# Eight half products and four small steps moved from ahead of the first attention to beside it, with the list steps of the last attention reordered

## The chip, the cores and the metric

The kernel runs on one core of one Trainium2 chip. The core has a matrix engine (PE, with its weight loads shown apart as PEld), a vector engine (DVE), a scalar engine (ACT), GpSimd (POOL) and a queue engine (SP) that issues most transfers. The metric is the device time of one execution in microseconds; less is better.

## The reference

The input is `x` (4 sequences of 512 tokens, 256 wide) and `cond_8` (4 by 8). All arithmetic is float32.

```
# 1. conditioned FFN: one of 8 experts for each sequence
e   = argmax(cond_8[b])
h   = silu(x[b] @ W_up[e].T + b_up[e]) * (x[b] @ W_gate[e].T + b_gate[e])   # 512 x 512
co  = h @ W_down[e].T + b_down[e]                                         # 512 x 256
# 2. attention with 16 query heads of 16 and one key/value head
q = (co @ Wq.T + bq) / 4;  k, v = split(co @ Wkv.T + bkv)
x = x + (softmax(q @ k.T) @ v) @ Wo.T + bo
# 3. a linear layer whose weight is mixed for each sequence
w_bot = sum_g cond_8[b, g] * weight[g] * mask
z = x @ w_bot.T + bias
# 4. mixture of 8 experts, two for each token, 128 places for each expert and group of 256 tokens
logits = z @ w_router;  probs = softmax(logits);  top 2
x = x + sum_e probs[e] * (gelu(z @ wi[e]) @ wo[e])     # places in order of choice, then token
```

The conditioned FFN's second product, `h @ W_down[e].T`, is what `down` computes. The mixed weight `w_bot` of each sequence is turned and multiplied by `w_router` once (`turn_mixed`, `route_mixed`), so that the logits come out of the same product as `z`.

## The kernel before, in words

The order of the work on every engine is the order of the program text; nothing rearranges it. Waits between engines come from the tiles that instructions share.

PSUM has eight banks of 128 x 512 floats in three groups: three `m`, one `a`, four `x` (`bank`). A product that wants a bank waits until the engine that reads the bank's last content is done.

**Ahead of the first attention.** For each sequence b and each quarter hc of the hidden width, `hidden(b, hc)` makes two products (lines 279 and 281), a silu on ACT (283) and an add and multiply on DVE (284) into the tile `hid`. `down(b, dc)` multiplies the whole of `hid` by one half of the output width (line 263, four products of 512 columns) and ACT adds the bias (264) into `coT`. `mixed` adds up the mixed weights on DVE (250, 252), four at a time. `keys`, `queries` and `values` project the sequence (313, 328, 335). For sequence 3, the last one, the four `hidden` and the `down` of sequences 2 and 3 stand in a table `before_steps`, together with turns (693) and routes (705) of the mixed weights: entry m runs after the maxima of step m, for m from 0 to 5. A large fill of the scatter buffer `xp` with zeros is issued from ACT's queue (361) just before.

**The attention steps.** 64 steps, 16 for each sequence, numbered n = 16 b + k. A step n handles the maxima of step n + 6 (`maxima`, four products at line 375 of 32 rows each, so that four fit the array side by side, and four DVE reductions, 379) and the exponentials of step n (`exponentials`, four products at 404 and four ACT exponentials, 408), and adds the weighted values of step n - 1 (`weigh`, line 422: products of 32 output columns, four side by side, accumulated in the `a` bank over four steps). After every fourth weighing the bank is copied out (431): by ACT, but by DVE for the last two units, 14 and 15. `shifted` turns the maxima (387) and sends them by four small transfers into rows of `q` (391). The last six steps (58 to 63) have no maxima left.

A step has one of two orders. Where the step's side work has PE products, it is called dense: half of the maxima and exponentials, the side work, the other half, then both halves of the weighing. Otherwise it is plain: half of the maxima and exponentials, half of the weighing, the other half of each, with the side work before the last half of the weighing.

**Side work.** The tables `beside` (sequences 0 to 2) and `last` (sequence 3) name, for each k, pieces of other sequences by their offset: projections of the next sequence, and of the previous ones the loads (`values`), the inverse sums (472), the residual bias (493, 128 x 1024 on DVE), the normalising (485), the output products (502, 507), turns (523), the mixed linear layer (534, 538), the choice of experts (`choose`, `rank0`, `rank1`, line 551 to 590), their places (`places`, `rows`, lines 600 to 631), `send` (637 to 649) and the scatter of rows to `xp` (`row0` to `row3`, line 655, two POOL transfers each). `bias` needs the residual rows that `residual` loads at steps 0, 27, 43 and 56.

In the last attention also stand the parts of `first_pairs`: lists of the first units of two tiles of 128 rows that belong to one expert (lines 826 to 879, some 14 to 18 small DVE instructions), the fetch of their weights (911) and rows (933), and the turn of unit 0 (975, 977).

**The experts.** Then come 25 units, of 256 or fewer rows each: `up` (1048, 1052), `put` (1081, 1091), and an accumulating scatter on POOL (1095). Weight tiles have three buffers. The pieces of the last sequence stand between the first units.

**Memory.** `hid` has two buffers in the pool `cp`, which is closed with `c1` ahead of the steps; the pools `ep`, `rp` and `fp` then take that room.

Of the kernel before, what the change touches and what calls it, by code (L numbers as in the profile page):

```python
# [10 lines left out]
F32 = mybir.dt.float32  # L11
# [6 lines left out]
P = 128  # L18
# [24 lines left out]
def adaln_attn_ffn_kernel(  # L43
# [77 lines left out]
    qp = attn_ctx.enter_context(tc.tile_pool(name="qp", bufs=2))  # L121
    c1 = ExitStack()
# [135 lines left out]
    def down(b, dc):  # L258
        w = w_of[b][1]
        wd = w[:, 0:1024].rearrange("p (c d) -> p c d", c=4)  # L260
        po = bank("x")
        for hc in range(4):
            mm(po, wd[:, hc, ts(dc, P)], hid_of[b][:, hc, :], start=hc == 0, stop=hc == 3)  # L263
        nc.scalar.activation(
            coT[:, dc, ts(b, T)], po, AF.Identity, bias=w[:, 1032 + dc : 1033 + dc]
        )

    def hidden(b, hc):
# [5 lines left out]
        if hc == 0:  # L274
            hid_of[b] = cp.tile([P, 4, T], F32, name="hid")
# [120 lines left out]
    def exponentials(n, js):  # L396
# [4 lines left out]
        for n4, j in enumerate(js):  # L401
            px = bank("m" if n4 >= 2 else "x")
# [10 lines left out]
    def weigh(n, js):  # L413
# [7 lines left out]
        for hh in range(4):  # L421
# [3 lines left out]
                start=sc == 0 and j0 > 0, stop=sc == 3 and j0 == 0,  # L425
# [273 lines left out]
    def route_mixed(b):  # L699
# [28 lines left out]
        [(-1, "bias"), (-2, "row1")],  # L728
# [8 lines left out]
        [],  # L737
# [6 lines left out]
        [(-1, "inv"), (0, "pairs0")],  # L744
        [(-1, "bias"), (-2, "send"), (-2, "row0")],
        [(-1, "norm0"), (-1, "norm1"), (-2, "row1")],
        [(-1, "out0"), (-1, "out1"), (-1, "out2"), (-1, "out3"), (-2, "row2")],
        [(-1, "rT0"), (-1, "rT1"), (-2, "row3")],
        [(-1, "mix0"), (-1, "mix1"), (-1, "mix2"), (-1, "mix3")],
        [(-1, "choose"), (-1, "rank0")],  # L750
        [(-1, "rank1"), (0, "pairs1")],
        [(-1, "places"), (-1, "rows"), (-1, "send"), (-1, "row0")],
        [(0, "values0"), (0, "pairs2"), (-1, "row1")],
        [(0, "pairs3"), (-1, "row2")],
        [(0, "bias"), (-1, "row3")],
        [(0, "pairs4")],
# [12 lines left out]

    def side(b, k):  # L770

        for off, name in (last if b == B - 1 else beside)[k]:
# [14 lines left out]

    before_steps = [
        [(hidden, B - 1, 0), (down, B - 2, 0)],
        [(down, B - 2, 1), (hidden, B - 1, 1), (turn_mixed, 0), (turn_mixed, 1)],  # L790
        [(hidden, B - 1, 2), (route_mixed, 0), (route_mixed, 1), (turn_mixed, 2)],
        [(hidden, B - 1, 3), (route_mixed, 2), (turn_mixed, 3)],
        [(down, B - 1, 0), (route_mixed, 3)],
        [(down, B - 1, 1)],
# [12 lines left out]
    fp = attn_ctx.enter_context(tc.tile_pool(name="fp", bufs=2))  # L807
# [8 lines left out]
    pairs = fp.tile([P, NE + 1], F32, name="pairs", bufs=1)  # L816
# [508 lines left out]
```

## Time and profile before

The median of 7 runs is 651.32 us (649.08 to 652.66). The profiled execution took 649.74 us, with a span of 647.9 us. The columns are busy times in us.

| stretch (us) | what runs | PE | DVE | ACT | DMA share |
|---|---|---|---|---|---|
| 0 to 69 | conditioned FFNs 0 to 2, first projections | 67.29 | 27.29 | 14.55 | 0.64 |
| 69 to 109 | FFN 3, `down` 2 and 3, turns, routes, maxima 0 to 5 | 40.00 | 24.16 | 7.06 | 0.71 |
| 109 to 171 | attention of sequence 0 | 62.00 | 42.19 | 39.74 | 0.13 |
| 171 to 239 | attention of sequence 1 | 68.00 | 47.23 | 38.13 | 0.24 |
| 239 to 306 | attention of sequence 2 | 66.96 | 50.57 | 36.93 | 0.28 |
| 306 to 361 | attention of sequence 3 to step 57 | 53.95 | 43.85 | 28.48 | 0.23 |
| 361 to 385 | steps 58 to 63, start of unit 0 | 21.63 | 14.69 | 15.24 | 0.66 |
| 385 to 625 | experts | 239.98 | 81.47 | 44.59 | 0.74 to 0.96 |
| 625 to 648 | last products and adds | 7.19 | 3.36 | 1.09 | 0.14 |

A product in float32 is two instructions on PE, so counts of PE instructions are twice those of products (transposes are single). The ends of PE instructions are modelled, and a PE instruction that is held up inside a group of products can look busy; the distance between the starts of the same instruction in two steps is the safer reading. In a line of the timeline, the bracket at the end gives the engine's idle time before it and what ended it.

### The profile page before, as it was taken

How to read it: one execution, taken by the hardware profiler on the slowest of the kernel's cores; microseconds unless marked ns; L12 is line 12 of the kernel's file. 1: busy time of each engine (PE TensorE's matmuls, PEld its weight loads, DVE VectorE, ACT ScalarE, POOL GpSimd, SP SyncE). 2: the span in 40 equal slices, each digit the busy share in tenths (PEclk: the TensorE clock that was granted, in tenths of full speed). 3: DMA queues.
4: the chain of work that ended last, by engine and by line, in shares of the span. 5: the costliest groups of instructions: out<-in, count | busy, mean ns of one | idle time of the engine just before them, and what ended most of it. 6: DMA issues, size and time to landing. Idle time of an engine off the chain costs nothing.

```text
span 647.9 us, 10621 instructions
## 1 busy us (share of the span) xinstructions
PE 627.0 (97%) x3968; PEld 373.2 (58%) x3968; DVE 334.8 (52%) x831; ACT 225.8 (35%) x404; POOL 111.3 (17%) x146
## 2 busy tenths in 40 slices
PE   8999999999999999999999999999999999999990
PEld 3444454333333433344335368888899999778880
DVE  1174844677668677876896853458222221322320
ACT  1212123566655455654553741221111111111220
POOL 1600000000000000310013051215342222223332
PEclk9999999999999999999999999999999999999996
DMA  6953981300142204321033299636889999898711
GB/s 232 379 146 71 310 268 34 98 19 18 34 133 68 67 18 119 133 70 47 19 97 122 95 344 305 220 99 197 249 270 324 315 340 318 249 278 256 215 20 19
DMA packets 65405, 107.14 MB, mean 165 GB/s; under 512 B 6914, under 2 KB 26946, under 8 KB 65346
## 3 DMA queue, kind: packets, MB, share of 16 engines
q1 hardware_dynamic: 50066, 87.96, 41.4%
q0 software_dynamic: 6400, 8.72, 6.8%
q10 hardware_dynamic: 8880, 9.71, 4.8%
q8 instruction: 33, 0.54, 0.3%
q14 instruction: 26, 0.21, 0.1%
HBM read 79.59 MB, written 26.65 MB: 164 GB/s over the span
## 4 chain that ended last, share of the span: by engine, by line
PE 91%; DVE 3%; DMA 2%; issue 1%; POOL 1%; SPq 0%; ACT 0%; POOLq 0%; DVEq 0%
PE ps_m L375 20%; PE ps_m L1048 17%; PE ps_x L1081 16%; PE ps_a L422 9%; PE ps_x L263 4%; PE ps_a L279 4%; PE ps_x L281 4%; PE ps_x L534 2%; PE ps_x L313 2%; PE ps_x L502 2%; PE ps_x L404 2%; PE ps_a L975 1%; PE ps_x L328 1%; PE ps_x L1015 1%; DVE negm L379 1%; PE ps_m L992 1%
## 5 line engine op out<-in xcount | busy, mean ns | idle before, releaser
L379 DVE TENSOR_REDUCE negm<-ps_m 128x1 f32<-128x512 f32 x250 | 160.7, 686 | 65.0 <-PE ps_x L404 43.1
L408 ACT ACTIVATE e<-ps_x 128x512 f32<-128x512 f32 x244 | 132.4, 594 | 106.0 <-PE ps_x L404 100.5
L375 PE MATMUL ps_m<-k,q 32*128 32x512 f32 x500 | 152.6, 639 | 0.4 <-DVE negm L379 0.3
L404 PE MATMUL ps_x<-q,k 32*128 32x512 f32 x488 | 138.9, 639 | 0.0
L1048 PE MATMUL ps_m<-xT,wi_sb 128*128 128x256 f32 (+1 forms) x672 | 115.4, 330 | 0.0
L1081 PE MATMUL ps_x<-wo_sb,e 128*128 128x256 f32 x512 | 114.3, 379 | 0.0
L1048 PEld LDWEIGHTS ps_m<-xT,wi_sb 128*128 128x128 f32 x672 | 103.7, 191 | 9.7 <-issue 0.4
L1081 PEld LDWEIGHTS ps_x<-wo_sb,e 128*128 128x128 f32 x512 | 95.6, 190 | 12.6 <-issue 0.4
L1052 ACT ACTIVATE e<-ps_m 128x512 f32<-128x512 f32 x64 | 38.0, 597 | 174.8 <-PE ps_m L1048 173.3
L1095 POOL DMA_INDIRECT out_dram<-y,to_row x36 | 55.5, 1542 | 137.1 <-DMA out_dram<-y,to_row 47.3
L375 PEld LDWEIGHTS ps_m<-k,q 32*128 32x128 f32 x500 | 46.4, 183 | 56.1 <-DVE negm L379 26.3
L422 PE MATMUL ps_a<-e,v 128*32 128x256 f32 x1024 | 75.8, 388 | 1.4 <-DVE cmp L826 1.4
L422 PEld LDWEIGHTS ps_a<-e,v 128*32 128x32 f32 x1024 | 23.2, 108 | 80.5 <-issue 64.0
L977 DVE COPY xT<-ps_a 128x256 f32<-128x256 f32 (+1 forms) x23 | 12.1, 528 | 82.1 <-PE ps_a L975 82.1
L1091 DVE TENSOR_SCALAR y<-ps_x,w 128x256 f32<-128x256 f32 x32 | 15.4, 483 | 58.8 <-PE ps_x L1081 58.7
L655 POOL DMA_INDIRECT xp<-x,to_i x32 | 33.2, 1038 | 57.6 <-DVE negm L379 29.7
L404 PEld LDWEIGHTS ps_x<-q,k 32*128 32x128 f32 x488 | 38.1, 182 | 2.1 <-issue 1.8
L584 POOL TENSOR_SCALAR x<-mk 128x4 f32<-128x4 f32 x4 | 0.8, 210 | 204.1 <-DVE mk L581 204.0
L284 DVE SCALAR_TENSOR_TENSOR hid<-ps_x,wo_sb,sg 128x512 f32<-128x512 f32 x16 | 12.0, 749 | 45.6 <-PE ps_x L281 45.6
L279 PE MATMUL ps_a<-xT_sb,wi_sb 128*128 128x512 f32 x64 | 30.5, 598 | 0.2 <-DMA wi_sb<-in_wcond_dram 0.2
L281 PE MATMUL ps_x<-xT_sb,wi_sb 128*128 128x512 f32 x64 | 30.1, 592 | 0.0
L263 PE MATMUL ps_x<-hid,wo_sb 128*128 128x512 f32 x64 | 28.8, 597 | 0.0
(166 smaller groups left out, 469.1 us busy)
## 6 DMA issues: line engine op xcount, KB each, us to landing
wi_sb<-in_wi_dram SPq DMA_DIRECT2D x25, 1024.0 KB
wo_sb<-in_wo_dram SPq DMA_DIRECT2D x25, 1024.0 KB
xp<-zeros ACTq DMA_DIRECT2D x1, 8712.0 KB
q<-qd SPq DMA_DIRECT2D x8, 512.0 KB
wi_sb<-in_wcond_dram SPq DMA_DIRECT2D x15, 256.0 KB
od<-stage SPq DMA_DIRECT2D x15, 256.0 KB
xt<-xp SPq DMA_DIRECT2D x11, 264.0 KB
wo_sb<-in_wcond_dram SPq DMA_DIRECT2D x4, 517.0 KB
```

What stands on the lines that cost most here:

```text
L263: mm(po, wd[:, hc, ts(dc, P)], hid_of[b][:, hc, :], start=hc == 0, stop=hc == 3)
L279: mm(pu, wu[:, c, :], xT_sb[:, c, ts(b, T)], start=c == 0, stop=c == 1)
L281: mm(pg, wg[:, c, :], xT_sb[:, c, ts(b, T)], start=c == 0, stop=c == 1)
L375: mm(pm, q[32 * j : 32 * j + 32, i, ts(hg, P)], k[32 * j : 32 * j + 32, :], start=True, stop=True,)
L379: nc.vector.tensor_reduce(nm[:, i, j : j + 1], pm, AX.X, ALU.max, negate=True)
L404: mm(px, k[rows_j, ts(sc, P)], seqs[u // 4]["q"][rows_j, :, ts(u % 4, P)], start=True, stop=True,)
L408: nc.scalar.activation(e_of[n][:, :, j, :].rearrange("p h (i t) -> p i h t", i=4), px.rearrange("p (i h t) -> p i h t", i=4, h=4), AF.Exp,)
L422: i = mm(pa_of[u][32 * hh : 32 * hh + 32, j0 * P : (j0 + nj) * P], seqs[b]["v"][:, sc, :], e[:, hh, j0 : j0 + nj].rearrange("p j n -> p (j ...
L1048: mm(ph[:, ts(k, n)], wi_of[u][:, c, ts(f0 + k, P)], xT_of[u][:, c, :], start=c == 0, stop=c == 1,)
L1052: nc.scalar.activation(hT_of[u][:, f0 : f0 + each].rearrange("p f t -> p (f t)"), ph, AF.Gelu_apprx_tanh,)
L1081: mm(po[:, 0:D], hT_of[u][:, fc, ts(h, P)], wo_of[u][:, fc, :], start=fc == 0, stop=fc == F // P - 1,)
L1095: i = nc.gpsimd.indirect_dma_start(out=out_rows, out_offset=bass.IndirectOffsetOnAxis(ap=to, axis=0), in_=y, in_offset=None, compute_op=AL ...
```

## The change

- `down` can take half of the tokens (256 columns). The eight halves of sequences 2 and 3 leave `before_steps` and stand in a table `halves` beside steps 3 to 9 and 11 of the first attention; the turns of the mixed weights of sequences 2 and 3 stand in step 12, their routes in step 13. These steps become dense.
- The hidden tiles of sequences 0 and 1 share one buffer; those of 2 and 3 get a pool `hp` of their own on the other side of the memory, closed at step 16. The pool `fp` and its first tiles are made there.
- In dense steps and in the last steps the weighing is one call over all four blocks of columns, products of 512 instead of 256 columns.
- In the steps without maxima the first two exponentials use `m` banks and the last two `x`, the other way round than before.
- The residual bias moves from step 5 of the next sequence (step 4 in the last attention) to step 14 of its own; that of the last sequence from 14 to 15.
- In `last`, `send` of sequence 1 moves from 4 to 3; the first list from 3 to 6; the second from 10 to 8; the fetches that stood with it stay at 10; `send` and `row0` of sequence 2 move from 11 to 12, `row1` from 12 to 13; the turn of unit 0 moves from 13 to 14.

```diff
@@ -119,6 +119,8 @@
     coT = apool.tile([P, 2, NT], F32, name="coT")
     wb_sb = apool.tile([P, B, 2, D + NE], F32, name="wb_sb")
     qp = attn_ctx.enter_context(tc.tile_pool(name="qp", bufs=2))
+    c2 = ExitStack()
+    hp = c2.enter_context(tc.tile_pool(name="hp", bufs=1, side="right"))
     c1 = ExitStack()
     cp = c1.enter_context(tc.tile_pool(name="cp", bufs=2))
     c1p = c1.enter_context(tc.tile_pool(name="c1p", bufs=1))
@@ -255,14 +257,20 @@
     mixing = [(b, g) for b in range(B) for g in range(NE)]
     hid_of = {}
 
-    def down(b, dc):
+    def down(b, dc, half=None):
+        n = T if half is None else T // 2
+        t0 = 0 if half is None else half * n
         w = w_of[b][1]
         wd = w[:, 0:1024].rearrange("p (c d) -> p c d", c=4)
-        po = bank("x")
+        po = bank("x")[:, 0:n]
         for hc in range(4):
-            mm(po, wd[:, hc, ts(dc, P)], hid_of[b][:, hc, :], start=hc == 0, stop=hc == 3)
+            mm(
+                po, wd[:, hc, ts(dc, P)], hid_of[b][:, hc, ds(t0, n)], start=hc == 0,
+                stop=hc == 3,
+            )
         nc.scalar.activation(
-            coT[:, dc, ts(b, T)], po, AF.Identity, bias=w[:, 1032 + dc : 1033 + dc]
+            coT[:, dc, ds(b * T + t0, n)], po, AF.Identity, bias=w[:, 1032 + dc : 1033 + dc]
         )
 
     def hidden(b, hc):
@@ -272,7 +280,11 @@
             for n in range(2)
         )
         if hc == 0:
-            hid_of[b] = cp.tile([P, 4, T], F32, name="hid")
+            hid_of[b] = (
+                cp.tile([P, 4, T], F32, name="hid", bufs=1) if b < B - 2
+                else hp.tile([P, 4, T], F32, name=f"hid{b}")
+            )
         pu = bank("a")
         pg = bank("x")
         for c in range(2):
@@ -399,7 +411,8 @@
         if n not in e_of:
             e_of[n] = ep.tile([P, 4, 4, P], F32, name="e")
         for n4, j in enumerate(js):
-            px = bank("m" if n4 >= 2 else "x")
+            px = bank("m" if len(js) == 4 and n4 < 2 else "x")
             rows_j = slice(32 * j, 32 * j + 32)
             mm(
                 px, k[rows_j, ts(sc, P)], seqs[u // 4]["q"][rows_j, :, ts(u % 4, P)],
@@ -422,7 +435,7 @@
             i = mm(
                 pa_of[u][32 * hh : 32 * hh + 32, j0 * P : (j0 + nj) * P], seqs[b]["v"][:, sc, :],
                 e[:, hh, j0 : j0 + nj].rearrange("p j n -> p (j n)"),
-                start=sc == 0 and j0 > 0, stop=sc == 3 and j0 == 0,
+                start=sc == 0 and js[-1] == 3, stop=sc == 3 and j0 == 0,
             )
         weighed.append(i)
         if sc == 3 and j0 == 0:
@@ -725,7 +738,7 @@
         [(-1, "values"), (1, "k"), (-2, "places"), (-2, "rows")],
         [(-2, "send")],
         [(-1, "inv"), (-2, "row0")],
-        [(-1, "bias"), (-2, "row1")],
+        [(-2, "row1")],
         [(-1, "norm0"), (-2, "row2")],
         [(-1, "norm1"), (-2, "row3")],
         [(-1, "out0"), (-1, "out1")],
@@ -734,26 +747,26 @@
         [(-1, "mix0"), (-1, "mix1")],
         [(-1, "mix2"), (-1, "mix3")],
         [(-1, "choose")],
-        [],
+        [(0, "bias")],
         [],
     ]
     last = [
         [(-2, "rank0")],
         [(-2, "rank1")],
         [(-1, "values"), (-2, "places"), (-2, "rows")],
-        [(-1, "inv"), (0, "pairs0")],
-        [(-1, "bias"), (-2, "send"), (-2, "row0")],
+        [(-1, "inv"), (-2, "send")],
+        [(-2, "row0")],
         [(-1, "norm0"), (-1, "norm1"), (-2, "row1")],
-        [(-1, "out0"), (-1, "out1"), (-1, "out2"), (-1, "out3"), (-2, "row2")],
+        [(-1, "out0"), (-1, "out1"), (0, "pairs0"), (-1, "out2"), (-1, "out3"), (-2, "row2")],
         [(-1, "rT0"), (-1, "rT1"), (-2, "row3")],
-        [(-1, "mix0"), (-1, "mix1"), (-1, "mix2"), (-1, "mix3")],
+        [(-1, "mix0"), (-1, "mix1"), (0, "pairs1"), (-1, "mix2"), (-1, "mix3")],
         [(-1, "choose"), (-1, "rank0")],
-        [(-1, "rank1"), (0, "pairs1")],
-        [(-1, "places"), (-1, "rows"), (-1, "send"), (-1, "row0")],
-        [(0, "values0"), (0, "pairs2"), (-1, "row1")],
-        [(0, "pairs3"), (-1, "row2")],
-        [(0, "bias"), (-1, "row3")],
-        [(0, "pairs4")],
+        [(-1, "rank1"), (0, "pairs2")],
+        [(-1, "places"), (-1, "rows")],
+        [(-1, "send"), (-1, "row0"), (0, "values0"), (0, "pairs3")],
+        [(0, "pairs4"), (-1, "row1"), (-1, "row2")],
+        [(0, "pairs5"), (-1, "row3")],
+        [(0, "bias"), (0, "pairs6")],
     ]
     ON_PE = ("q", "k", "v", "out", "rT", "mix")
 
@@ -767,8 +780,21 @@
     STEPS = 16 * B
     work = {b: finish(b) for b in range(B)}
 
+    halves = {
+        k: [(down, b, dc, half)]
+        for k, (b, dc, half) in zip(
+            (3, 4, 5, 6, 7, 8, 9, 11), itertools.product((B - 2, B - 1), range(2), range(2))
+        )
+    }
+    halves[12] = [(turn_mixed, 2), (turn_mixed, 3)]
+    halves[13] = [(route_mixed, 2), (route_mixed, 3)]
     def side(b, k):
 
+        for f, *of in halves.get(k, ()) if b == 0 else ():
+            f(*of)
         for off, name in (last if b == B - 1 else beside)[k]:
             to = b + off
             if not 0 <= to < B:
@@ -784,14 +810,9 @@
                 work[to][name]()
 
 
     before_steps = [
-        [(hidden, B - 1, 0), (down, B - 2, 0)],
-        [(down, B - 2, 1), (hidden, B - 1, 1), (turn_mixed, 0), (turn_mixed, 1)],
-        [(hidden, B - 1, 2), (route_mixed, 0), (route_mixed, 1), (turn_mixed, 2)],
-        [(hidden, B - 1, 3), (route_mixed, 2), (turn_mixed, 3)],
-        [(down, B - 1, 0), (route_mixed, 3)],
-        [(down, B - 1, 1)],
+        [(hidden, B - 1, 0)], [(hidden, B - 1, 1)], [(hidden, B - 1, 2)], [(hidden, B - 1, 3)],
+        [(turn_mixed, 0), (turn_mixed, 1)], [(route_mixed, 0), (route_mixed, 1)],
     ]
     for m in range(LEAD):
         maxima(m, (0, 1, 2, 3))
@@ -804,7 +825,6 @@
     c1.close()
     ep = attn_ctx.enter_context(tc.tile_pool(name="ep", bufs=2))
     rp = attn_ctx.enter_context(tc.tile_pool(name="rp", bufs=2))
-    fp = attn_ctx.enter_context(tc.tile_pool(name="fp", bufs=2))
 
 
 
@@ -813,12 +833,6 @@
     UHALF = NA + NB + NTILE
     UQUARTER = UHALF + NE
     NUNIT = UQUARTER + NE
-    pairs = fp.tile([P, NE + 1], F32, name="pairs", bufs=1)
-    nc.gpsimd.memset(pairs, 0.0)
-    texp = fp.tile([P, NUNIT], F32, name="texp", bufs=1)
-    table = fp.tile([P, 2, NUNIT], I32, name="table", bufs=1)
-    count = fp.tile([P, 1], I32, name="count", bufs=1)
     def of_experts(t, less, op, begin):
 
         n = begin.shape[2]
@@ -949,17 +963,19 @@
             next(parts[0])
         elif part == "1":
             next(parts[0], None)
+        elif part == "2":
             fetch_in(0)
             fetch_rows(0)
             fetch_rows(1)
-        elif part == "2":
+        elif part == "3":
             for _ in list_of_pairs(N0, NA - N0):
                 pass
-        elif part == "3":
+        elif part == "4":
 
             i = fetch_in(1)
             tc.add_manual_dep(i.ins, weighed[-1].ins.name, AFTER, reason="not at once")
             fetch_out(0)
+        elif part == "5":
             turn(0, "x")
         else:
             i = fetch_in(2)
@@ -1119,21 +1135,29 @@
 
     for n in range(STEPS + 1):
         m = n + LEAD
+        if n == 16:
+            c2.close()
+            fp = attn_ctx.enter_context(tc.tile_pool(name="fp", bufs=2, side="right"))
+            pairs = fp.tile([P, NE + 1], F32, name="pairs", bufs=1)
+            nc.gpsimd.memset(pairs, 0.0)
+            texp = fp.tile([P, NUNIT], F32, name="texp", bufs=1)
+            table = fp.tile([P, 2, NUNIT], I32, name="table", bufs=1)
+            count = fp.tile([P, 1], I32, name="count", bufs=1)
         if n in (0, 27, 43, 56):
             residual((0, 27, 43, 56).index(n))
         b, k = divmod(n, 16)
         names = [name for _, name in (last if b == B - 1 else beside)[k]] if b < B else []
         dense = any(
             name.rstrip("0123") in ON_PE and (b > 0 or name in projection[0]) for name in names
-        )
+        ) or (b == 0 and k in halves)
         if m >= STEPS:
             if n < STEPS:
                 exponentials(n, (0, 1, 2, 3))
             if n == STEPS:
 
                 up(0, 0)
-            weigh(n - 1, (2, 3))
-            weigh(n - 1, (0, 1))
+            weigh(n - 1, (0, 1, 2, 3))
             if n < STEPS:
                 side(b, k)
         elif dense:
@@ -1146,8 +1170,7 @@
             if m % 4 == 3:
                 shifted(m // 4)
             if n > 0:
-                weigh(n - 1, (2, 3))
-                weigh(n - 1, (0, 1))
+                weigh(n - 1, (0, 1, 2, 3))
         else:
 
             maxima(m, (0, 1))
```

## The prediction

> **What bounds the kernel now.** I read the page's busy line first, then the same busy times by stage, then the PE timeline of single steps, and last the stretch where PE has gaps.
>
> ```profile
> span 647.9 us, 10621 instructions
> PE 627.0 (97%) x3968; PEld 373.2 (58%) x3968; DVE 334.8 (52%) x831; ACT 225.8 (35%) x404; POOL 111.3 (17%) x146
> ```
>
> Columns of the next view: stretch, its length, then busy time and count on PE, PEld, DVE, ACT, POOL, the granted clock, DMA share and GB/s.
>
> ```profile
> 69.00:109.00 40.00, 40.00 (x164) 19.42 (x160) 24.16 (x43) 7.06 (x11) 0.11 (x1) 1.00 0.71 225
> 109.00:171.00 62.00, 62.00 (x514) 21.97 (x515) 42.19 (x69) 39.74 (x72) 0.00 (x0) 1.00 0.13 40
> 306.00:361.00 55.00, 53.95 (x432) 21.67 (x432) 43.85 (x102) 28.48 (x55) 8.99 (x11) 1.00 0.23 75
> 361.00:385.00 24.00, 21.63 (x191) 10.43 (x192) 14.69 (x74) 15.24 (x29) 9.44 (x11) 1.00 0.66 223
> 468.00:555.00 87.00, 87.00 (x574) 80.58 (x577) 19.78 (x79) 14.33 (x24) 22.78 (x26) 1.00 0.96 303
> ```
>
> 69 to 109 is the stretch ahead of the first attention, 109 to 171 the first attention, 306 to 385 the last one. PE is the bound nearly everywhere; only the last attention has open gaps. So what counts is PE time removed, PE time added, and the gaps. Busy PE can hide a wait inside a modelled matmul, so steps are read by their period. A plain step of the first attention, then a dense one of the second:
>
> ```profile
> 134.53 0.90 PE L375 MATMUL ps_m<-k,q 32*128 32x512 f32 x2
> 135.81 0.64 PE L422 MATMUL ps_a<-e,v 128*32 128x256 f32 x8
> 136.38 0.75 PE L375 MATMUL ps_m<-k,q 32*128 32x512 f32 x2
> 137.50 0.64 PE L422 MATMUL ps_a<-e,v 128*32 128x256 f32 x8
> 138.07 0.91 PE L375 MATMUL ps_m<-k,q 32*128 32x512 f32 x2
> ...
> 210.21 0.70 PE L375 MATMUL ps_m<-k,q 32*128 32x512 f32 x2
> 211.28 1.99 PE L502 MATMUL ps_x<-wo_sb,attn 128*128 128x256 f32 x8
> 213.20 0.70 PE L375 MATMUL ps_m<-k,q 32*128 32x512 f32 x2
> 214.27 1.07 PE L422 MATMUL ps_a<-e,v 128*32 128x256 f32 x16
> 215.27 0.70 PE L375 MATMUL ps_m<-k,q 32*128 32x512 f32 x2
> ```
>
> Starts give the periods: plain 138.07 - 134.53 = 3.54 us; dense 215.27 - 210.21 = 5.06 us, of which the side slot is 213.20 - 211.28 = 1.92 us (eight passes of 256 columns). Without side work a dense step is 3.14 us.
>
> The gaps of the last steps:
>
> ```profile
> 371.75 1.07 PE L422 MATMUL ps_a<-e,v 128*32 128x256 f32 x16 [1.35 <-DVE cmp L826]
> 373.84 0.66 PE L975 MATMUL ps_x<-ident,xt 128*128 128x128 f32 x4 [1.02 <-DMA xt<-xp]
> ```
>
> ```profile
> 370.92 0.68 DVE L431 COPY stage<-ps_a 128x512 f32<-128x512 f32 x1
> ```
>
> The first gap is PE waiting for the single `a` bank, which DVE empties late (370.92) because lists and ranks are queued ahead of the copy. The second is the turn of the first unit waiting for its rows.
>
> **1. Out of the head.** Between the first maxima (68.28) and step 0 (108.92) PE has no gap. Leaving: four `down` of 3.53 us (72.89 to 76.42) = 14.1; the turns of sequences 2 and 3, 0.57 + 0.56 = 1.1; their routes, 0.81 + 0.88 = 1.7. Sum 16.9 us. What is late next is DVE: its 24.16 us in that stretch stay but for two copies of 0.17, against 23.7 us left on PE. Followed step by step: the first reduces run 71.58 to 74.05, then the hidden product to 74.7, then four mixing products to 77.7. The second maxima find their third `m` bank 0.5 us late, the third maxima (wanted at 77.9, banks at 78.3 to 79.5) lose 1.4 us, the sixth 0.6 us. So step 0 starts near 94.5, not 108.92: **-14.4**. Ends: -16.9 (no stall) and -11.9 (twice the stall).
>
> The shifted maxima of unit 0 (four DMAs, 2.49 us of issue on SP) would go out at about 88.2, and the exponentials of step 0 want them at 94.5. They now run beside the zero fill of `xp`, whose DMA share is 1.09 until 92 and 0.05 after 94. No row shows a small transfer under that fill; an unloaded one released its reader 1.45 us after issue (ivd at 194.60, inv at 196.05). If it lands normally the cost is 0, if it waits for the fill to end, about 94 + 1.5 - 94.5 = 1 us. I take 0, since 3.8 us of slack stand behind the last issue at 90.7.
>
> [...]
>
> **2. Into the first attention.** A half `down` is four products of 256 columns in two passes: the same eight passes as the dense step shown. Width costs nothing: 32 passes of 256 columns take 6.91 us (0.216 each), eight of 512 take 3.43 (0.429). Steps 3 to 9 and 11 go from 3.54 to 5.06: 8 x 1.52 = 12.2, less 0.15 because step 8 took 3.69, less 0.2 because step 10 (4.17) follows a dense step. Step 12 with two turns (eight transposes, 1.02 us as in the chain's L523 x8): 3.14 + 1.05 = 4.2, and 0.15 for ACT, which has four exponentials (2.17), two copies and the `a` copy (0.59 each) there, 3.9 in all: +0.8. Step 13 with two routes: 3.14 + 1.8 = 4.95, +1.4. ACT's evictions of a half are off the path: in the q and k steps (5.06 too) ACT has a 0.69 us eviction.
>
> The residual bias, 1.18 us on DVE, comes to step 14. In the second attention it stood at 197.92 behind a 0.31 us transpose and made the next step 4.50 instead of 3.54 (196.96 to 201.46). Without the transpose I take 0.96 - 0.31 = 0.65. Its input landed long before. Sum of part 2: 12.2 - 0.35 + 0.8 + 1.4 + 0.65 = **+14.7**. Ends: 13.5 (steps 12 to 15 hide their additions) and 16.7 (0.2 more in each of ten steps, which is what a dense step shows between 5.06 and its 5.16 forms, twice over).
>
> [...]
>
> **3. Merged weighing.** 39 calls take four products of 512 columns instead of eight of 256. Two halves back to back take 1.00 us, one half 0.57: 0.43 of streaming each and 0.14 once. The merged call streams the same 0.86 and pays 0.14 once: **0**. Ends -0.05 and +0.03 each, -2 to +1.
>
> **4. Bias of sequences 1 and 2** leaves a step with a transpose for one without: -0.3 each, **-0.6**.
>
> **5. Last attention to the outputs.** Steps 49 to 53 (316.37 to 338.21 by their groups) take 21.8 us against 17.7 plain: DVE holds them. DVE loses the bias (1.22) and the first list (0.85), 2.07 us; `send` only moves one step earlier. The freed room falls into a step that PE then bounds at 3.54, so I take half: **-1.0** (0 to -2.07). The second list, 2.4 us of small DVE work, now stands between the mixes, where DVE shows gaps of only 0.37, 0.46 and 0.46: +0.3.
>
> **6. Last six steps.** From 360.83 PE needs 2.07 us a step plus 0.59 each for places and turn. Over that it lost 0.88 at step 59 and 0.76 at step 63 (the fourth exponential's product waits for an `m` bank whose exponential is third in ACT's line; with `m` given to the first two, its releaser is first in line), and 3.3 around step 61, the two gaps shown with it. Sum 4.9. After: the `a` copy stands ahead of `send` and of the second list, so the bank is free at about 368.8, when PE wants it at 369.1; the table is written two steps earlier, so SP, which sits until 367.50, issues the weights near 364.5 and the rows near 366.4; with the 4.41 us of the chain's row transfer they land near 370.8, and the turn now stands one step later (about 372). What stays is ACT, 2.17 us a step, worth 0.6. **-4.3** (-1.35, the copy alone, to -4.9). SP's output of unit 14 and the later loads queue behind these fetches, which are earlier. The scatters of sequence 2 gain only 1.7 us (`send` ends near 370.2, eight POOL issues of 1.3 us), so the third unit's rows may be late: +0.3.
>
> **No cost.** The first two hidden tiles share a buffer, so DVE's product (1,0) waits for both `down` of sequence 0: from 25.1 to 31.9. Behind it on DVE is only the product at 35.40, with 9.56 us idle before it; its `x` bank is next wanted at 36.9. Without that idle it would cost its 0.75. The `pairs` memset on POOL moves to step 16, long before its reader.
>
> **Sum.** -14.4 + 14.7 + 0 - 0.6 - 1.0 + 0.3 - 4.3 + 0.3 = -5.0. The profiled execution took 649.74 (span 647.9 and 1.84 around it): 644.7. It lay 1.6 below the median 651.32; for the median I give 646.3. A measurement tells about 0.2%, 1.3 us, from no change.
>
> **Rivals.**
> *The tail keeps its waits* (row transfer or ACT last): only 1.35 of 4.9 goes, -2.0 in all, 649.3. For: ACT at 2.17 against PE's 2.07 a step. Against: ACT idles 3.86 us before 375.65.
> *The experts swallow the gain:* from 468 the DMA share is 0.96, and if the weight stream sets the end, all but the first units' earlier start is lost: 651. Against: PE 87.00 of 87.00; fetches start when PE frees a buffer, so both move together.
> *Slower: the first attention's new dense steps are dearer than those of the second.* Five `x` banks are asked for per step where four exist. Each of ten steps must lose 0.5 us (5.56) before the gain is gone; at 0.7 it is 653.3. For: the mixing steps with two banks show 5.16. Against: 5.06 with the same pattern in q and k steps.
>
> **How the numbers follow.** Forecast 0.55 (own range 643.5 to 649), tail 0.19, experts 0.10, slower 0.16. Faster: 0.55 and most of the tail case, 0.72; same: 0.10; slower: 0.18. The range leaves out 0.1 at each end: 642.8 with the head's best end (-2.5) and half of part 5; 652.0 inside the slower case.
>
> **What would show it.** Right: step 0 near 94.5, first attention about 76.5 us long, steps with a half `down` at 5.06, no PE gap above 1 us after 361. Wrong: step 0 waiting on DVE or on q's rows, dense steps above 5.3, the first `up` not near 14 us after step 58 starts (18.5 before: 360.83 to 379.33).

## The result, and the profile after

The kernel after takes 647.52 us in the median of 17 runs (646.43 to 649.88); the kernel before, run beside it, 650.69 us. The ratio is 0.9955, with a 95% interval of 0.9946 to 0.9964: faster by 0.45%, some 2.9 us, where 5.0 were forecast. The profiled execution took 646.92 us against 649.74, spans 645.2 and 647.9.

The page of the kernel after, its span and busy times:

```profile
span 645.2 us, 10051 instructions
PE 625.6 (97%) x3688; PEld 366.9 (57%) x3688; DVE 334.3 (52%) x831; ACT 226.9 (35%) x408; POOL 110.8 (17%) x146
```

Its busy times by stage, in the columns of the stage view of before:

```profile
69.00:95.00 26.00, 25.88 (x105) 11.43 (x97) 23.13 (x39) 3.82 (x6) 0.00 (x0) 1.00 1.08 336
95.00:174.00 79.00, 79.00 (x506) 32.05 (x509) 44.25 (x76) 43.89 (x81) 0.11 (x1) 0.98 0.12 35
307.00:362.00 55.00, 53.99 (x409) 20.86 (x405) 45.56 (x116) 28.70 (x55) 9.03 (x11) 1.00 0.23 75
362.00:382.00 20.00, 19.42 (x134) 7.90 (x134) 12.80 (x60) 15.38 (x30) 8.16 (x11) 1.00 0.66 225
466.00:553.00 87.00, 87.00 (x575) 80.59 (x578) 19.81 (x79) 14.34 (x24) 22.78 (x26) 1.00 0.97 303
```

Two things stand out. In the first row DVE is busy for 23.13 of 26 us: it is now the near bound of the head. In the second row the granted clock is 0.98, not 1.00: for a part of the first attention PE ran at a lower clock. The open gaps of the last steps have shrunk (19.42 of 20 us, before 21.63 of 24), and the experts are as they were.

The steps with a half `down`, in the PE timeline of the kernel after:

```profile
112.35 0.70 PE L387 MATMUL ps_m<-k,q 32*128 32x512 f32 x2
...
113.42 1.99 PE L268 MATMUL ps_x<-hid,wo_sb 128*128 128x256 f32 x8
115.34 0.70 PE L387 MATMUL ps_m<-k,q 32*128 32x512 f32 x2
...
117.41 0.70 PE L387 MATMUL ps_m<-k,q 32*128 32x512 f32 x2
```

117.41 - 112.35 = 5.06 us a step and 1.92 us for the side slot (115.34 - 113.42), both as forecast.

The last steps, PE and DVE (step 58 starts at 361.93):

```profile
370.81 1.07 PE L435 MATMUL ps_a<-e,v 128*32 128x512 f32 x8
...
373.87 0.66 PE L991 MATMUL ps_x<-ident,xt 128*128 128x128 f32 x4
...
376.69 3.72 PE L1064 MATMUL ps_m<-xT,wi_sb 128*128 128x256 f32 x16
...
381.34 0.66 PE L991 MATMUL ps_x<-ident,xt 128*128 128x128 f32 x4
...
393.18 0.66 PE L991 MATMUL ps_a<-ident,xt 128*128 128x128 f32 x4 [0.82 <-DMA xt<-xp]
```

```profile
369.68 0.69 DVE L444 COPY stage<-ps_a 128x512 f32<-128x512 f32 x1
```

The waits of 1.35 us (the `a` bank) and 1.02 us (the first turn) are gone: the copy runs at 369.68 and the weighing at 370.81 finds its bank. The first `up` comes 376.69 - 361.93 = 14.76 us after step 58 starts, against 18.50 before and 14 forecast. But the third unit's turn, at 393.18, now waits 0.82 us for its rows; before, that turn started at 395.01 with no wait. The same places in the kernel before (step 0, step 58, first `up`, third turn):

```profile
108.92 0.70 PE L375 MATMUL ps_m<-k,q 32*128 32x512 f32 x2
...
360.83 0.70 PE L404 MATMUL ps_x<-q,k 32*128 32x512 f32 x2
...
379.33 3.72 PE L1048 MATMUL ps_m<-xT,wi_sb 128*128 128x256 f32 x16
...
395.01 0.66 PE L975 MATMUL ps_a<-ident,xt 128*128 128x128 f32 x4
```

Set against the prediction's terms, by the starts of the same instructions in the two profiled executions:

| place | forecast | measured |
|---|---|---|
| head: step 0 at 95.50 instead of 108.92 | -14.4 | -13.4 |
| first attention without the clock | +14.7 | +14.4 |
| lowered clock in it | not in the sum | +1.7 |
| attentions of sequences 1 and 2 | -0.6 | -0.9 |
| last attention to step 58 | -0.7 | -0.7 |
| last six steps to the first `up` | -4.3 | -3.7 |
| third unit's rows | +0.3 | +0.8 |
| last output transfers | 0 | -0.9 |
| sum | -5.0 | -2.7 |

The last output is taken as chance: one of the last scatters on POOL stood 3.74 us behind the transfer before it in the execution of before, and in that of after 2.89 us, for its input alone; in the profiles of e1 to e8 below this wait lies between 2.59 and 3.16 us.

The clock in the stretch from the first row of the table to the second, columns as above:

```profile
96.00:97.00 1.00, 1.00 (x9) 0.27 (x2) 0.35 (x1) 0.16 (x1) 0.00 (x0) 0.92 0.05 21
97.00:98.00 1.00, 1.00 (x2) 0.48 (x2) 0.94 (x2) 1.00 (x1) 0.00 (x0) 0.50 0.00 0
98.00:99.00 1.00, 1.00 (x2) 0.35 (x2) 0.00 (x0) 0.99 (x3) 0.00 (x0) 0.50 0.00 0
99.00:100.00 1.00, 1.00 (x2) 0.00 (x0) 0.00 (x0) 0.22 (x1) 0.00 (x0) 0.50 0.00 0
100.00:101.00 1.00, 1.00 (x9) 0.42 (x9) 0.00 (x0) 0.55 (x1) 0.00 (x0) 0.88 0.00 0
```

```profile
96.73 3.68 PE L325 MATMUL ps_x<-coT,wq_sb 128*128 128x512 f32 x4
103.31 1.98 PE L325 MATMUL ps_x<-coT,wq_sb 128*128 128x512 f32 x4
```

From about 96.9 to 100.2 the granted clock is 0.50. The first half of the projection q takes 3.68 us, the second, the same work at full clock, 1.98: 1.7 us. Just ahead of it stand the two routes, 20 PE instructions (ten products) of 8 columns in 2.33 us, and before them the waits shown next.

The profiled execution of before showed no such fall until after its last product, and its granted clock averaged 0.992. The profiles of this case tie this average to the falls: 0.992 goes with no fall ahead of the kernel's end (before, e3, e8), 0.988 to 0.990 with one, 0.982 to 0.987 with several or a longer one. Most runs of before lie at 0.985 to 0.989, those of after at 0.983 to 0.990, so by these averages such falls belong to most executions of both. The three runs of before at 0.992 on one chip took 648.9 to 649.2 us, 1.1 under the median there (650.2). The kernel after without its fall would take 646.9 - 1.7 = 645.2, 2.3 under its median; e5, which runs as the kernel after, took 645.0 and 645.2 in its two runs at 0.992. So falls cost the median about 1.2 us more after than before, an estimate; the profiled pair shows the whole 1.7.

The head of the kernel after, PE:

```profile
73.02 1.22 PE L387 MATMUL ps_m<-k,q 32*128 32x512 f32 x3
...
78.42 1.89 PE L387 MATMUL ps_m<-k,q 32*128 32x512 f32 x5
...
91.10 1.70 PE L387 MATMUL ps_m<-k,q 32*128 32x512 f32 x5
...
93.17 1.06 PE L718 MATMUL ps_x<-wr_sb,stage 128*128 128x8 f32 x8
...
94.53 1.04 PE L718 MATMUL ps_x<-wr_sb,stage 128*128 128x8 f32 x8
95.50 0.70 PE L387 MATMUL ps_m<-k,q 32*128 32x512 f32 x2
```

Maxima that wait for nothing take 0.70 us for the first group and 1.06 in all. Here the second are 0.5, the third 1.2 and the sixth 1.0 us longer: PE waits for `m` banks that DVE has not reduced yet, inside what the rows show as busy.

### The profile page after: what moved, and what is told of

Same layout as the page of the kernel before. It is cut to its first block, busy times and chain, and to the rows that moved or that the text cites. A ratio compares the mean times of both kernels' runs of the same rounds, so it can differ in the third digit from the quotient of the medians.

```text
span 645.2 us, 10051 instructions
## 1 busy us (share of the span) xinstructions
PE 625.6 (97%) x3688; PEld 366.9 (57%) x3688; DVE 334.3 (52%) x831; ACT 226.9 (35%) x408; POOL 110.8 (17%) x146
## 4 chain that ended last, share of the span: by engine, by line
PE 91%; DMA 3%; DVE 2%; POOL 1%; issue 1%; ACT 0%; SPq 0%; POOLq 0%; DVEq 0%
PE ps_m L387 21%; PE ps_x L1097 17%; PE ps_m L1064 16%; PE ps_a L435 10%; PE ps_x L268 5%; PE ps_a L291 4%; PE ps_x L293 4%; PE ps_x L325 3%; PE ps_x L547 2%; PE ps_x L515 2%; PE ps_x L417 1%; PE ps_a L991 1%; PE ps_x L340 1%; DMA xp<-x,to_i 1%; PE ps_x L1031 1%; DMA xt<-xp 1%
## 5 line engine op out<-in xcount | busy, mean ns | idle before, releaser
L435 PE MATMUL ps_a<-e,v 128*32 128x256 f32 (+1 forms) x712 | 73.5, 485 | 0.5 <-ACT e L421 0.2
L435 PEld LDWEIGHTS ps_a<-e,v 128*32 128x32 f32 x712 | 14.0, 108 | 67.2 <-issue 57.2
L268 PE MATMUL ps_x<-hid,wo_sb 128*128 128x256 f32 (+1 forms) x96 | 30.0, 459 | 0.0
L295 ACT ACTIVATE sg<-ps_a,wo_sb 128x512 f32<-128x512 f32 x16 | 11.0, 687 | 49.1 <-PE ps_a L291 41.6
```

Source lines behind the costliest of these rows:

```text
L268: mm(po, wd[:, hc, ts(dc, P)], hid_of[b][:, hc, ds(t0, n)], start=hc == 0, stop=hc == 3,)
L435: i = mm(pa_of[u][32 * hh : 32 * hh + 32, j0 * P : (j0 + nj) * P], seqs[b]["v"][:, sc, :], e[:, hh, j0 : j0 + nj].rearrange("p j n -> p (j ...
```

## The experiments

All but the last four were timed on two chips where the kernel before took 650.2 to 650.3 us.

**Take the exchange back, keep the rest (e1), and the exchange alone (e2).** e1 is the kernel after with the head of before; e2 is the kernel before with the exchange and what it needs.

```
# e1                                   # e2: before, and
-    halves = { ... }                  +    halves = { ... }
+    halves = {}                       +    before_steps = [ ... as after ... ]
+    before_steps = [ ... as before ]  +    down by halves, hid in its own pool
```

> The changed kernel with its head put back: the eight half products and the four turn and route steps return to the places of before, whole; everything else of the change stays. Theory A (the exchange between head and first attention loses, the last attention gains): the first side product of step 16 moved by +2.7 us in the changed kernel, of which 0.4 is the bias at step 14, so the exchange alone costs about 2.2 us, and this kernel takes 647.5 - 2.2 = 645.3 (ratio to the kernel before 0.992), with a granted clock of 1.00 all through the head. Theory B (the exchange is neutral, as the prediction's terms -14.4 and +14.1 say, and the miss lies elsewhere): 647.2 to 647.5, ratio 0.995.

> The kernel before with the exchange alone: halves of the two last second products, turns and routes beside the first attention, the hidden tiles' pools, nothing of the weighing, the banks of the last steps, the bias or the last attention's table. Theory A: 650.7 + 2.2 = 652.9, ratio 1.0034, and the gaps of 1.35 and 1.02 us after step 58 are still there. Theory B: 650.4, ratio 0.9995. A third case, the exchange carries the gain: 648, ratio 0.996.

e1: 645.45 us (644.53 to 646.38), ratio 0.9923 (0.9910 to 0.9936). e2: 653.18 us (650.56 to 655.2), ratio 1.0039 (1.0024 to 1.0054). The two agree: the exchange, which gives the change its name, costs 2 to 2.5 us, and the reordered lists, banks and biases bring about 5. The prediction had -0.35 for the exchange (-14.4 + 14.05) and -4.65 for the rest.

I had expected a clock of 1.00 all through the head of e1. Its profile, with the head of before, shows the same fall, behind the same two routes (89.81 to 91.96), where no maxima had waited:

```profile
93.00:94.00 1.00, 1.00 (x9) 0.03 (x1) 0.00 (x0) 0.22 (x1) 0.00 (x0) 0.58 0.52 162
94.00:95.00 1.00, 1.00 (x6) 0.48 (x3) 0.96 (x2) 0.00 (x0) 0.00 (x0) 0.50 0.06 20
```

```profile
91.07 1.04 PE L718 MATMUL ps_x<-wr_sb,stage 128*128 128x8 f32 x8
...
93.97 3.26 PE L291 MATMUL ps_a<-xT_sb,wi_sb 128*128 128x512 f32 x4
```

So the shortened head is not needed for the fall. With one fall of 3.4 us in each profile, e1 starts q of sequence 1 at 173.83, the kernel after at 174.91, and the spans are 644.3 and 645.2: at equal clock the exchange costs about 1 us. The rest goes, by the run clocks, with falls that come more often: three of the five runs of e1 have a clock of 0.991 or 0.992, none of the kernel after, and e2's eight lie at 0.980 to 0.988.

**Fill the waits of the head (e3, e8).** Where PE waits in the head, a whole `down` costs less than its 3.5 us. e3 takes the two whole `down` of sequence 2 back into the head, ahead of the third maxima and of the turns; e8 puts them ahead of the second maxima and between the two routes.

```
# e3
-        [(hidden, B - 1, 0)], [(hidden, B - 1, 1)], [(hidden, B - 1, 2)], [(hidden, B - 1, 3)],
-        [(turn_mixed, 0), (turn_mixed, 1)], [(route_mixed, 0), (route_mixed, 1)],
+        [(hidden, B - 1, 0)], [(hidden, B - 1, 1), (down, B - 2, 0)], [(hidden, B - 1, 2)],
+        [(hidden, B - 1, 3)], [(down, B - 2, 1), (turn_mixed, 0), (turn_mixed, 1)],
+        [(route_mixed, 0), (route_mixed, 1)],
# e8
+        [(hidden, B - 1, 0), (down, B - 2, 0)], [(hidden, B - 1, 1)], [(hidden, B - 1, 2)],
+        [(hidden, B - 1, 3), (turn_mixed, 0), (turn_mixed, 1)],
+        [(route_mixed, 0), (down, B - 2, 1)], [(route_mixed, 1)],
# both: the halves of sequence 3 alone stay, in steps 3 to 6
-            (3, 4, 5, 6, 7, 8, 9, 11), itertools.product((B - 2, B - 1), range(2), range(2))
+            (3, 4, 5, 6), itertools.product((B - 1,), range(2), range(2))
```

> The changed kernel with the second products of sequence 2 kept whole in the head, after the hidden products of entries 1 and ahead of the turns in entry 4, where PE waited for DVE; only the four halves of sequence 3 go beside steps 3 to 6. Theory A (the head lost 3 us to waits for DVE and 1.7 us to a lowered clock, and PE work in those places costs little): head +7.06 less about 2.3 of waits and 1.7 of clock, first attention -6.1: 647.5 - 3.0 = 644.5, ratio 0.9905, clock 1.00 through the head. If the clock falls all the same: 646.2, ratio 0.993. Theory B (waits stay what they are): 647.5 + 1.0 = 648.5, ratio 0.9965.

> The changed kernel with half of its exchange taken back, where the head has waits: the two whole down of sequence 2 go back ahead of the first attention (one after the first hidden product, one between the two routes) and only the four halves of sequence 3 stand beside the first attention, in its steps 3 to 6. My theory: a whole down in the head costs 3.53 less the wait that it covers, two halves cost 2 x 1.52 = 3.0 in the attention, so the exchange itself is nearly even and the waits of 2.5 us in the head decide; with the routes parted the clock has no long stretch of narrow products before step 0: 644.0 us, ratio 0.990. Rival (filling the waits is all that counts, and how the routes lie counts nothing): 644.7 as the other filling gave, ratio 0.991. Second rival (the head's waits are only modelled): 647.5, ratio 0.995.

e3: 644.67 us (643.92 to 646.89), ratio 0.9920 (0.9906 to 0.9935). e8: 643.84 us (643.01 to 644.37), ratio 0.9903 (0.9889 to 0.9917). Both are as expected, and e8 beats both kernels: its five runs all have a clock of 0.991 or 0.992, which no run of after reaches. Its head:

```profile
76.67 0.71 PE L387 MATMUL ps_m<-k,q 32*128 32x512 f32 x3
...
81.37 0.70 PE L387 MATMUL ps_m<-k,q 32*128 32x512 f32 x3
...
99.75 1.14 PE L387 MATMUL ps_m<-k,q 32*128 32x512 f32 x3
...
101.46 1.98 PE L325 MATMUL ps_x<-coT,wq_sb 128*128 128x512 f32 x4
```

The maxima that waited are at 0.70 again; a smaller wait is left in step 0 (1.14 for its first group), and q runs at full clock. q of sequence 1 starts at 172.09, in the kernel after at 174.91: 2.8 us, of which 1.7 are the clock and 1.1 what the shorter waits bring after the price of the moved work. The two effects are separated only in this way, by the rows; e3, with the routes still together, showed no fall in its profile either, so where the routes lie is not shown to be the cause.

**Dense work between the routes (e4).** Two products that nobody reads stand between the routes.

```
-        [(turn_mixed, 0), (turn_mixed, 1)], [(route_mixed, 0), (route_mixed, 1)],
+        [(turn_mixed, 0), (turn_mixed, 1)],
+        [(route_mixed, 0), (idle_products, 2), (route_mixed, 1)],
```

> The changed kernel with two idle products (128 x 512, results read by nobody, 1.72 us of PE) between the two routes of the head. Theory A (the granted clock fell to 0.50 for 3.4 us at the start of the first attention because PE streamed hardly any columns during the routes): the clock stays at 1.00, 1.7 us come back, and the kernel takes 647.5 + 1.72 - 1.7 = 647.5, ratio 0.995. Theory C (the fall has another cause, such as the table load or the exponentials' start): it falls all the same and the kernel takes 649.2, ratio 0.998.

647.02 us (646.35 to 654.96), ratio 0.9956 (0.9940 to 0.9973): as the kernel after, with 1.7 us of idle work added. Six of eight runs have a clock of 0.990 to 0.992 and lie at 646.4 to 647.2; the other two, at 0.986 and 0.982, took 650.4 and 655.0. The last is the profiled one, and shows falls at 94, 166 and 398: the first begins in the first route, ahead of the dense products, the second behind the routes of step 13, the third in a PE wait of 3.51 us for the third unit's rows. So by the run clocks the dense products often keep the fall away, not always.

**Weighing in halves again (e5).**

```
-            weigh(n - 1, (0, 1, 2, 3))
+            weigh(n - 1, (2, 3))
+            weigh(n - 1, (0, 1))
```

> The changed kernel with the weighing of the second half of the steps split again into two calls of 256 columns, as in the kernel before; all else stays. My theory (merging is worth nothing, the streamed columns are the same and two halves followed each other in 1.00 us as the merged call does): 647.5 us within 1.3, ratio 0.995. Rival (the merging saved 0.05 us in each of 39 calls): 649.5, ratio 0.998. Second rival (four queued products of 512 columns hold the next exponential's bank longer than two by two): faster, 646.5.

647.05 us (644.95 to 651.65), ratio 0.9955 (0.9937 to 0.9972), exactly that of after. Merging is worth nothing, as forecast. Its profiled run, 4.7 us slower than the kernel after's, has the third unit's wait at 3.66 us instead of 0.82, and the clock falls right behind it (396 to 400).

**Banks back (e6), tables back (e7).**

```
# e6
-            px = bank("m" if len(js) == 4 and n4 < 2 else "x")
+            px = bank("m" if n4 >= 2 else "x")
# e7: beside, last and the parts of first_pairs as in the kernel before
```

> The changed kernel, in whose last six steps the fourth-quarter products take their banks again in the order of the kernel before (m for the last two, not for the first two). The lists keep the changed order. My theory: the waits of 0.88 and 0.76 us for an m bank come back, 647.5 + 1.6 = 649.1 us, ratio 0.9975. Rival (the waits came from the lists ahead of them, and their order alone took them away): 647.5, ratio 0.995.

> The changed kernel with the three tables of side work as before from the residual bias on: bias, table send, lists and the turn of the first unit stand where they stood in the kernel before, and the first list goes beside the last attention's early steps. The bank order and the head's exchange stay. My theory: the terms of the bias (0.9 - 0.4), of the last attention to the outputs (0.7) and of the two gaps of 1.35 and 1.02 us with what they draw on (2.1 to 2.4) are undone: 647.5 + 3.3 = 650.8 us, ratio 1.000, with PE gaps above 0.8 us near the lists' copy and the turn. Rival (the bank order carried the tail): 648.5, ratio 0.9965, gaps under 0.5 us.

e6: 647.29 us (646.12 to 649.93), ratio 0.9961 (0.9948 to 0.9974). I expected 649.1, and the rival's 647.5 came out, though not for its reason. PE in the profile of e6:

```profile
382.25 0.66 PE L991 MATMUL ps_x<-ident,xt 128*128 128x128 f32 x4
393.18 0.66 PE L991 MATMUL ps_a<-ident,xt 128*128 128x128 f32 x4
```

The bank order does count: with the old one the first `up` comes 15.64 us after step 58 instead of 14.76, and the second turn stands at 382.25 instead of 381.34. But the third turn is at 393.18 in both: the kernel after comes there earlier and waits 0.82 us for the rows, e6 shows no such wait on PE, and the 0.9 us are gone.

The rows' own chain in the kernel after, from its POOL and SP timelines:

```profile
372.31 1.04 POOL L668 DMA_INDIRECT xp<-x,to_i  x1 [6.15 <-DVE cmp L848]
...
381.78 0.98 POOL L668 DMA_INDIRECT xp<-x,to_i  x1 [0.30 <-issue]
```

```profile
387.81 0.38 SPq L947 DMA_DIRECT2D xt<-xp  x1
```

Eight scatters of 1.29 us each, then SP issues the fetch. In the kernel before the first scatter started at 371.88 and the fetch at 387.68: nothing of this chain became earlier, since `send` now stands behind the copy of the `a` bank. Whether the scatters alone set when the rows land is not shown: e6 issued the fetch at 388.37, 0.56 us later than the kernel after, and its turn starts at the same time.

e7: 653.57 us (651.86 to 654.61), ratio 1.0059 (1.0046 to 1.0071), against 650.8 expected. The two gaps are back, as its PE timeline shows:

```profile
375.33 1.06 PE L435 MATMUL ps_a<-e,v 128*32 128x512 f32 x8 [1.28 <-DVE cmp L840]
377.09 0.66 PE L989 MATMUL ps_x<-ident,xt 128*128 128x128 f32 x4 [0.70 <-DMA xt<-xp]
```

From step 58 to the first `up` it takes 17.59 us: 2.8 of the 3.7 us won there belong to the tables, 0.9 to the banks. With 1.2 us in the attentions of sequences 1 and 2 and 0.5 in the last one, that is 4.5 us, 1.2 more than expected. The measured difference to the kernel after is 6.5 us (against e5, which runs as the kernel after); the other 2 go with its clock, 0.981 to 0.987 in all runs, an argument and no measurement; in the profiled one, the fastest, the fall in the head lasts 6.8 us instead of 3.4.

**An earlier send (e9 to e12).** To bring the third unit's rows forward, e9 takes e8 and moves `send` and the first scatters ahead of the copy; e10 also takes the old banks.

```
-        [(-1, "places"), (-1, "rows")],
-        [(-1, "send"), (-1, "row0"), (0, "values0"), (0, "pairs3")],
+        [(-1, "places"), (-1, "rows"), (-1, "send"), (-1, "row0")],
+        [(0, "values0"), (0, "pairs3")],
```

> The kernel of the second filling (e8) with the send of sequence 2 and its first two scatters moved one step earlier, to stand behind the ranks and ahead of DVE's copy of the a bank; the copy comes some 1.06 us later, the scatters 1.06 us earlier. Theory R (after the change the turn of the third unit waits for its rows, 0.8 us in the profiled execution, because the last of the eight scatters that these rows wait for comes no earlier than before): PE loses about 0.6 us in front of the late a bank and gets back the 0.8 us wait, so 643.6 us, ratio 0.990 against 0.9903 of e8, with no wait of PE for the third unit's rows in the profile. Rival (the wait for the rows is a wait for the queue of weights ahead of them, not for the scatters): 644.4, ratio 0.991, the wait still there.

> As e9_send_early, and the bank order of the kernel before in the last six steps. With the late scatters the bank order was worth 0.9 us up to the first up and nothing at the end, since the third unit waited for its rows. Theory R: with the rows early it counts again in part: 644.2 us, ratio 0.991, that is 0.6 (0.3 to 0.9) above e9 of the same call. Rival (the bank order costs nothing anywhere in the end): as e9.

e9: 649.35 us, ratio 0.9945 (0.9924 to 0.9967); e10: 649.97 us, ratio 0.9952 (0.9933 to 0.9971), on a chip where before took 652.69 us. The third unit's wait is gone, but in e9 a wait of 0.95 us for the `a` bank has come (0.18 in e10), and in both profiles PE waits some 4.2 us ahead of the first `up`, because ACT, DVE and SP stand still together. With PE that late, the missing wait says nothing of the rows: e11 below shows none either, without the earlier send. So both kernels of e8 and e9 were run once more on one chip:

> The kernel of e8 once more, beside that of e9, since e9 was measured on another chip, on which the kernel before took 652.7 us instead of 650.2, and its profile shows ACT, DVE and SP all standing still from about 372 to 378 us. Theory chip (the stand-still comes with that chip, whatever the edit): this kernel has ratio 0.990 where its profile shows no such stand-still and 0.994 where it does. Theory edit (the earlier send brings the stand-still): ratio 0.990 and no stand-still on any chip.

> The kernel of e9 once more on the same chip as e11. Theory chip: within 0.5 us of e11, with or without the stand-still as e11 has it. Theory edit: the stand-still of about 6 us is there again and this kernel is 2.5 to 4 us slower than e11.

Before took 653.19 us here. e11: 647.16 us (645.42 to 649.19), ratio 0.9901 (0.9877 to 0.9925), as in its first measurement. e12: 649.52 us (649.36 to 650.23), ratio 0.9946 (0.9925 to 0.9967). e11 falls into two groups, 645.4 to 646.0 and 648.3 to 649.2, three runs each, and its profiled run is of the slower group. Its ACT, DVE and PE:

```profile
377.96 1.08 ACT L421 ACTIVATE e<-ps_m 128x512 f32<-128x512 f32 x2 [6.04 <-remote]
```

```profile
376.47 0.69 DVE L994 COPY xT<-ps_x 128x512 f32<-128x512 f32 x1 [4.60 <-remote]
```

```profile
377.22 5.34 PE L1065 MATMUL ps_m<-xT,wi_sb 128*128 128x256 f32 x16 [3.62 <-issue]
```

The stand-still comes with e8 too, so the earlier send does not make it; all runs of e12 (649.4 to 650.2) lie at or just above e11's slower half, so it may make it the rule. Neither theory holds as written. What the three engines wait for, the trace does not name ("remote"), and it stays open; so does what an earlier send is worth without it. That the rows' wait takes back the banks' gain at the third unit rests on e6.

## Why the prediction was right, and where it was not

The sign and the range held (646.3 forecast, 642.8 to 652.0); the gain was 2 us smaller.

1. *Out of the head*, -14.4: measured -13.4, inside its ends. DVE was late next where the prediction said, at the second, third and sixth maxima: 0.5, 1.2 and 1.0 us against 0.5, 1.4 and 0.6, and 0.2 in a hidden product. The work that stays took 24.25 us (six maxima of 1.06, four hidden steps of 3.63, turns 1.04, routes 2.33) instead of 23.7. The transfers beside the zero fill cost nothing, as taken: their issue grew to 4.02 us,

```profile
88.37 4.02 SPq L403 DMA_DIRECT2D q<-nmT  x4
```

but the exponentials of step 0 started at 95.68 with no wait for them in the trace, while the DMA share was still 0.70.

2. *Into the first attention*, +14.7: measured +14.4 at full clock; steps at 5.06, step 12 at 4.43 (4.35 forecast), step 13 at 5.02 (4.95), the bias 0.43 instead of 0.65. The rival of dearer dense steps fell.

The step that failed is that parts 1 and 2 were summed as if PE kept its clock: the granted clock was 1.00 in all rows that I had read, and I did not ask why that execution lay 1.6 us under the median. The clock falls to 0.50 for 3.4 us behind the routes, 160 columns with no dense product between, and the profile shows the 1.7 us that this costs. The place is firm: the fourteen profiles have nine falls with no gap on PE, and each begins between 1.1 us after the first product of a group of routes and 1.4 us after its last, be it in the head (e1 with the old head too) or in step 13 (e4, e10). The other seven ahead of the kernel's end begin in or just behind PE gaps of 3.5 to 4.3 us, or in e2 between two of 1.1 and 1.4 us. That the narrow products are the cause is argued: before and e3 escaped in their profiles with the routes together, and no run is without routes. The kernel after has two such places with two routes together, in the head and in step 13, where before has one; that this is why the falls come more often is an idea that no run tests.

Apart from the clock, parts 1 and 2 together came out 0.7 us dearer (+1.0 for +0.3). Of the 2 us by which the medians missed the forecast, the estimate above puts 1.2 on the clock.

All sixteen falls ahead of the kernel's end last 3.4 us or twice that (6.8 us), and by the average clocks (0.982 to 0.992 among the runs of e5) a fall comes in some runs of a kernel and not in others. PE's rows are busy throughout in nine of them. What sets the length, and what makes the clock fall where PE's rows show no gap, the runs do not show.

3. *Merged weighing*, 0: confirmed by e5.

4, 5. *Biases, last attention to the outputs*, -0.6 and -0.7: -0.9 and -0.7. The output products at step 54 wait 0.82 us for DVE where they waited 0.48; the rest came as summed.

6. *Last six steps*, -4.3: -3.7, 2.8 from the tables and 0.9 from the banks. Waits of 0.24 and 0.20 us are left where 0.6 was allowed. *The tail keeps its waits* fell. *Third unit's rows*, +0.3, was sized wrongly: I had `send` end near 370.2, with scatters 1.7 us earlier, but they came 0.4 us later, and the wait is 0.8. *The experts swallow the gain* was right in a place where I had not put it: the wait for these rows takes back the banks' share.

*No cost.* The shared `hid` buffer made DVE's second product wait to 31.99 us, as summed, behind 9.54 us in which DVE had nothing else to do; PE's products there start within 0.1 us of before.

## What to carry to other kernels

When work leaves a stretch, ask what the bound engine does in the time that remains: a whole product left in a wait for the next engine was cheaper than the same work by halves elsewhere (e8 against the kernel after: 2.8 us less up to sequence 1, 1.7 of them the clock). A profile at full clock is no fair pair for one with a fall: compare the average clock of the runs before a small difference is put down to the edit. Before a gain far from the end is counted, look for the next transfer whose start did not move, and take the gain only up to it.

## What the runs showed of the hardware

- PE's granted clock fell to 0.50 for 3.4 or 6.8 us, nine times in fourteen profiles with no gap in PE's busy rows, always within 1.4 us of a group of products of 8 columns; by the average clocks (0.985 to 0.989 in most runs of before, 0.983 to 0.990 in those of after) such falls are in most runs of either kernel. One fall at a dense projection cost 1.7 us (3.68 against 1.98). Six PE gaps of 3.46 to 4.25 us ahead of the kernel's end (e4, e5, e9 to e12) each had a fall at their end. Falls explain much of the spread: the runs of e5 go from 645.0 us at a clock of 0.992 to 651.3 at 0.982.
- Four small transfers took 4.02 us to issue beside the zero fill of `xp`, 2.49 without it.
- On two chips where the kernel before took 2.5 to 3 us more, ACT, DVE and SP stood still together, ACT and DVE for 4.6 to 6.1 us from about 372 to 374 us, with POOL and the transfers going on; by the run times e8 had it in half of its runs there, and its profile on the other chip not at all.
